# A planner that counts eight transfers in flight, with four of its durations changed, in a four-layer graph network

## The chip, the cores and the metric

The kernel runs on one core of one Trainium2 chip. The metric is the device time of one execution in microseconds (us); smaller is better. All data are 32-bit floats. In the profile PE is TensorE's matmuls, PEld its loads of weights, DVE VectorE, ACT ScalarE, POOL GpSimd, and SP SyncE, whose queue issues nearly all DMA transfers.

## The reference

128 graphs of 128 nodes with 512 features pass four layers. Each layer is `x = layernorm(x + f(x, adj))`, with another `f`; `adj` is a sparse 128 x 128 matrix for each graph. Cut to what matters:

```python
# layer 0: graph convolution over K = 3 hops, with attention weights
Xw = X @ Wv + bv
e = leaky_relu(sj[:, None, :] + si[:, :, None] + ab)         # sj, si: Xw @ aw
alpha = A * exp(e);  T = alpha / (alpha.sum(-1) + 1e-12)
for k in range(3):
    H = H + Xk @ Wk[k] + bk[k];  Xk = T @ Xk                 # f = relu(H)
# layer 1: two hypergraph convolutions, 512 -> 1024 -> 512
def conv(x, adj, W, b):                                      # H = adj != 0
    return Dn * (H @ (Be * (H.T @ (x @ W.T)))) + b           # Dn, Be: 1 / weighted degrees
h = layer_norm(relu(conv(x, adj, W1, b1))) * gamma + beta;  f = conv(h, adj, W2, b2) + x
# layer 2: tanh attention
s = (x @ w) @ a;  A = exp(leaky(8 * tanh((s_i + s_j) / 8))) * adj
A = A / A.sum(-1) * adj.sum(-1);  f = A @ x @ w
# layer 3: 8 heads of 64, scores times the mask 2 * adj, softmax
q, k, v = proj(x);  S = softmax(q @ k.T / 8 * (adj + adj));  f = (S @ v) @ Wo.T + bo
```

## The kernel before

**A program that is planned before it is issued.** The kernel's code does not issue instructions as it runs. Every call such as `ve.tensor_tensor(...)` goes to `Plan.add`, which notes the engine, an estimated duration (`estimate`), a key (`plan.key`, a due time in units of a pair of graphs), and on which earlier operations it depends. Some 90,000 instructions come out of it. At the end `Plan.emit` orders all of them, and each engine runs its own list strictly in that order. Since all instructions are issued from one line of `emit` (L375), the profile has one line for all; operations are told apart by the names of the buffers (`four`, `out`, `first`, `side`, `sq`, `bank`, `t`) that they write and read.

**How `Plan.order` works.** It is a list scheduler with a clock for each of the five engines. In each step it takes, for each engine, the operations whose inputs are ready; `look(e)` gives each the time `t` at which it could start, and among those that could start within `SLACK` = 60 ns of the earliest it takes the one of best rank. The rank is the key in the first pass; in two further passes it is a deadline worked back from the first pass's start times, for all engines but TensorE. Of the three orders the one with the shortest planned time is issued. An operation that takes a new buffer also needs a free slot in SBUF or PSUM, so the plan chooses the buffers too. An operation in a `plan.together()` block is planned as one piece: its durations are added, times a share given to `together`.

**Transfers in the plan.** A DMA keeps its queue for `ISSUE` = 450 ns an instruction; its data then go over one common pipe (`pipe`), 1000 ns (`BEGIN`) after the issue at the earliest, for a time worked out from the bytes and the runs (`o[7]`); operations that need the data become ready 2300 ns after the pipe's end (the last row of `LATENCY`). In the issued program, transfers use eight semaphores in turn, and each waits, in its issuing queue, until the transfer eight places ahead has landed. The plan before has no such limit.

**Ports in the plan.** An operation of POOL, or of DVE with two SBUF operands, shares a port (`shares_port`). When POOL ends, DVE's port is held `YIELD` = 20 ns longer.

**The stages.** Work goes in steps of two pairs of graphs (`both`), so 32 steps a layer. Large products are done by Strassen's method (`strassen`, and twice over in `twice`). In layer 0, the weighted `e` goes through DRAM to be turned (`through_dram`: writes in groups of four pieces of 16 KB, `e<-sq`, then one load, `sq<-e`), and the same is done in layer 1 with `h` and in layers 2 and 3 with `F`, `x` and `S`. Layer 1 loads `adj` in groups of four pieces (`sq<-in_adj_dram`) and counts nonzeros with `ve.tensor_scalar(..., accum_out=cnt)`. Layers 2 and 3 run in one function (`layer23`), which calls `attention`; it has 16 matmuls of scores in one `together` block (two of them on the upper and lower 64 rows of the array) and 16 matmuls with the values in another (two on halves of the columns). `dot` is a multiply-add on VectorE with `accum_out`, both operands in SBUF.

While layer 0 runs, the weights of later layers are combined and parked in DRAM (`park_49`, `park_7`: `w1s`, `w2s`, `qks` and others). Between the layers they are loaded into `first` (`take_49`, `take_w2`), a buffer that the weights of the layer before used, seven loads of 896 KB or 512 KB in a row.

Of the kernel before, what the change touches and what calls it, by code (L numbers as in the profile page):

```python
# [59 lines left out]
PE, DVE, ACT, POOL, SP = range(5)  # L60

LATENCY = ((0, 205, 215, 255, 300), (225, 120, 110, 200, 200), (160, 145, 140, 200, 200), (110, 140, 100, 105, 200),
           (2300, 2300, 2300, 2300, 2300))
ISSUE, BEGIN = 450, 1000
EARLY = -0.5
QW = 3 * P + 2
SLACK = 60
SPARE, AHEAD = 4, 6
YIELD = 20
SIZE = {"four": U * D, "sq": U * (P + 2), "bank": D, "col": 12, "row": D, "w28": 7168, "q7": 7 * 2 * P,  # L70
        "w7": 7 * QW, "out": U * 4 * QW, "t0": D, "t1": D, "row1": 4 * D, "k": U * (P + 2),
        "prep": U * D}
# [51 lines left out]
def estimate(engine, name, out, args, kw):  # L124

    n = out.idx.size if isinstance(out, View) else 0
    views = [a for a in args if isinstance(a, View)]
    psum = any(a.tile.kind in PSUM for a in views)
    scalars = sum(isinstance(a, View) and a.idx.size == 1 for k, a in [*enumerate(args), *kw.items()] if k != "accum_out")
    if engine == PE:  # L130
        return 107 if name == "transpose" else (1.74 if n <= P else 1.68) * n
    if name == "dma_start":
        return ISSUE
    if engine == DVE:
        if name == "bn_aggr":
            return 95
        if name == "reciprocal":
            return 67 + 6.5 * n
        if name in ("tensor_reduce", "bn_stats"):
            n = views[0].idx.size  # L140
        fast = name in ("tensor_scalar", "tensor_copy") and not psum and "accum_out" not in kw
        return 67 + n / (1.92 if fast else .96) + (61 * scalars if n > 8 else 0)
    if engine == ACT:
        return 50 + n / 1.2 + (0 if psum else 43) + 92 * scalars + 94 * ("accum_out" in kw)
    if name == "tensor_tensor":
        return 500 + 35 * n if OP.pow in args else 150 + 2.1 * n if n < 800 else 1.82 * n
    return 60 if name == "memset" else 180 + 3.2 * n if n > 8 else 215


def shares_port(engine, name, args, kw):  # L150
# [22 lines left out]
class Plan:  # L173
# [64 lines left out]
    def order(self, urgent=None):  # L238


        ops = self.ops
        n = len(ops)
        after = [[] for _ in range(n)]
        left = [len(o[4]) for o in ops]
        todo, first = {}, {}
        for k, o in enumerate(ops):
            for d in o[4]:
                after[d].append(k)
            for t in o[5]:
                todo[t] = todo.get(t, 0) + 1  # L250
                first[t] = min(first.get(t, o[3]), o[3])
        line = {kind: sorted((t for t in first if t.kind == kind), key=first.get, reverse=True) for kind in self.slots}
        slots = {kind: [(0, i) for i in range(m)] for kind, m in self.slots.items()}
        place = {}
        later = {new: (set(old), 0.0) for new, old in self.later.items()}

        def settle(kind):

            if line[kind] or kind not in {old[0] for olds in self.later.values() for old in olds}:
                return False  # L260
            found, slots[kind] = slots[kind], []
            for at, i in found:
                for new, (old, when) in list(later.items()):
                    if (kind, i) in old:
                        later[new] = rest, when = old - {(kind, i)}, max(when, at)
                        if not rest:
                            slots[new[0]].append((when, new[1]))
            return bool(found)

        rank = [o[3] if o[0] == PE or urgent is None else (urgent[k], k) for k, o in enumerate(ops)]  # L270
        ready = [{} for _ in range(5)]
        come, free, start = [0.0] * n, [0.0] * 5, [0.0] * n
        port = [0.0] * 5
        pipe, reached = 0.0, EARLY
        for k in range(n):
            if not left[k]:
                ready[ops[k][0]][k] = 0.0

        def look(e):

            can = []
            soonest = math.inf
            for k, t in ready[e].items():
                if e == SP and ops[k][8] > reached and not ops[k][4]:
                    continue
                t = max(t, free[e], port[e] if ops[k][6] else 0)
                new = {}
                for tile in ops[k][5]:
                    if tile not in place:
                        new.setdefault(tile.kind, []).append(tile)  # L290
                for kind, tiles in new.items():
                    s, m = slots[kind], len(tiles)
                    spare = 0
                    if not all(tile in line[kind][-m:] for tile in tiles):
                        spare = SPARE if all(tile in line[kind][-m - AHEAD:] for tile in tiles) else math.inf
                    if len(s) < m + (min(spare, 4) if kind == "bank" else spare):
                        break
                    t = max(t, sorted(s)[m - 1][0])
                else:
                    can.append((rank[k], t, k))  # L300
                    if t < soonest:
                        soonest = t
            if not can:
                return None
            r, t, k = min(c for c in can if c[1] <= soonest + SLACK)
            return t, k

        best = [look(e) for e in range(5)]
        count = 0
        while count < n:  # L310
            t, e = min((b[0], e) for e, b in enumerate(best) if b)
            k = best[e][1]
            o = ops[k]
            stale = {e}
            for tile in o[5]:
                if tile not in place:
                    s, l = slots[tile.kind], line[tile.kind]
                    at = min(s) if tile.place is None else next(x for x in s if x[1] == tile.place)
                    s.remove(at)
                    place[tile] = at[1]  # L320
                    l.remove(tile)
                    settle(tile.kind)
                    stale = set(range(5))
            del ready[e][k]
            start[k] = t
            free[e] = end = t + o[2]
            if o[7]:
                end = pipe = max(pipe, t + BEGIN) + o[7]
            if e == PE and o[8] > reached:
                reached = o[8]  # L330
                stale.add(SP)
            if o[6]:
                port[DVE + POOL - e] = end + (YIELD if e == POOL else 0)
                stale.add(DVE + POOL - e)
            count += 1
            for tile in o[5]:
                todo[tile] -= 1
                if not todo[tile]:
                    slots[tile.kind].append((end + max(LATENCY[SP if o[7] else e]), place[tile]))
                    settle(tile.kind)  # L340
                    stale = set(range(5))
            for j in after[k]:
                f = ops[j][0]
                come[j] = max(come[j], end + LATENCY[SP if o[7] else e][f])
                left[j] -= 1
                if not left[j]:
                    ready[f][j] = come[j]
                    stale.add(f)
            for f in stale:
                best[f] = look(f)  # L350
        return start, place, max(free)
# [32 lines left out]
def kernel(  # L384
# [14 lines left out]
    psum = ctx.enter_context(tc.tile_pool(name="psum", bufs=1, space=PS))  # L399
# [40 lines left out]
    plan = Plan(slots, later)  # L440
# [1015 lines left out]
    def attention(i0, A, qT, kT, v, x3d, base, r):  # L1456
# [4 lines left out]
        Ss = [four().rearrange("p u (j a) -> p (u j) a", a=Q).rearrange("p (k j) a -> p k j a", k=4)  # L1461
              for _ in range(U)]
        ps = [[bank(), bank()] for _ in range(U)]
        with plan.together(.65):
            for b in range(U):
                for i in range(C):
                    for r2 in range(2):
                        pe.matmul(ps[b][r2][:, i * P:(i + 1) * P],
                                  qT[r2 * HD:(r2 + 1) * HD, b, i],
                                  kT[r2 * HD:(r2 + 1) * HD, b, i], start=True, stop=True)  # L1470
# [33 lines left out]
            PTs.append(PT)  # L1504
        cT = four().rearrange("p u (i n) -> p u i n", n=P)
        ps = [bank() for _ in range(U)]
        with plan.together(.62):
            for b in range(U):
                for i in range(C):
                    for r2 in range(2):  # L1510
                        hh = (2 * i + r2) * HD
                        pe.matmul(ps[b][r2 * HD:(r2 + 1) * HD, i * P:(i + 1) * P], v[:, b, hh:hh + HD],
                                  PTs[b][:, r2, i * P:(i + 1) * P], start=True, stop=True)
        for b in range(U):
            ac.copy(cT[:, b].rearrange("p i (r m) -> p i r m", m=4), rows_in_order(ps[b]))
        ops = operands(*blocks(cT))
# [8 lines left out]
    n = B // U  # L1525
# [61 lines left out]
```

## Time and profile before

| what | value |
|---|---|
| runs | 5402.33, 5396.24, 5395.81 us; median 5396.24 |
| profiled execution | 5406.97 us, its span 5405.0 us |
| granted TensorE clock | 0.998 |
| busy PE / DVE / POOL / ACT | 5324.9 / 4410.1 / 3913.6 / 2387.5 us |
| DMA | 813.70 MB, mean 151 GB/s |
| instructions | 93,824 |

The page's "busy" time of an engine is the time in which at least one of its instructions runs; an instruction's record reaches somewhat into the next one's, since engines are pipelined. A 32-bit matmul has two records, one for each of its passes. In groups of instructions, the first numbers after the bar are total busy time and mean ns of one, then follow the idle time of the engine just before them and what ended it. A line of the waits gives total us, the number of waits and the longest. In the timeline the columns are start, length in us, engine, operation with buffers, and in brackets the engine's idle time before it with its releaser.

### The profile page before, as it was taken

The numbers are of one execution on the slowest core, as the hardware profiler recorded it, in microseconds if no ns is written. First come the engines' busy times: TensorE is split into PE (matmuls) and PEld (weight loads), VectorE is DVE, ScalarE is ACT, GpSimd is POOL, SyncE is SP. The second block draws the span as 40 slices with busy tenths as digits, with TensorE's granted clock in tenths as the row PEclk, the third lists the DMA queues.
The fourth block names the chain that finished last, engine by engine and source line by source line (L and its number), as shares of the span: only waits on it lengthen the run. The fifth ranks groups of instructions, "written<-read, shape, count | busy, mean of one in ns | idle before, by whom it ended". The sixth has DMA issues, their size and how long they took to land.

```text
span 5405.0 us, 93824 instructions
## 1 busy us (share of the span) xinstructions
PE 5324.9 (99%) x29039; PEld 4239.3 (78%) x29039; DVE 4410.1 (82%) x11721; ACT 2387.5 (44%) x6085; POOL 3913.6 (72%) x4937
## 2 busy tenths in 40 slices
PE   8999999999999999999999999999999999999998
PEld 4555555555788888888888889988988998998987
DVE  7788888887888888888888777878777878788886
ACT  3343333343444444444444444444444444444444
POOL 6777677676676767676767577777777777778776
PEclk9999999999999999999999999999999999999999
DMA  4444444435554545454554745555555555555543
GB/s 112 134 135 130 130 146 134 128 113 181 154 157 145 158 146 158 147 157 146 157 150 146 246 137 158 159 154 161 162 154 158 157 161 156 162 154 163 156 153 109
DMA packets 842412, 813.70 MB, mean 151 GB/s; under 512 B 269612, under 2 KB 642868, under 8 KB 841912
## 3 DMA queue, kind: packets, MB, share of 16 engines
q1 hardware_dynamic: 838914, 806.65, 49.2%
q8 instruction: 231, 3.78, 0.3%
q14 instruction: 269, 2.20, 0.1%
q10 hardware_dynamic: 2998, 1.06, 0.1%
HBM read 458.38 MB, written 349.04 MB: 149 GB/s over the span
## 4 chain that ended last, share of the span: by engine, by line
PE 87%; DVE 5%; DMA 3%; issue 1%; SPq 1%; ACT 1%; POOL 1%; ACTq 0%; DVEq 0%; POOLq 0%
PE bank L375 66%; PE t L375 21%; DVE out L375 1%; SPq L375 1%; DVE col L375 1%; DVE four L375 1%; DMA first<-x3d 1%; DMA four<-in_x_dram 1%; ACT out L375 0%; DMA out<-x3d 0%; DMA sq<-e 0%; POOL out L375 0%; DVE junk L375 0%; DVE first L375 0%; DMA sq<-in_adj_dram 0%
## 5 line engine op out<-in xcount | busy, mean ns | idle before, releaser
L375 PE MATMUL bank<-first,four 128*128 128x386 f32 (+2 forms) x6008 | 1735.6, 433 | 27.3 <-DVE out L375 11.4
L375 PEld LDWEIGHTS bank<-first,four 128*128 128x128 f32 (+1 forms) x6008 | 1073.0, 189 | 600.6 <-DVE out L375 119.2
L375 DVE TENSOR_TENSOR out<-bank,out 128x386 f32<-128x386 f32 (+1 forms) x2089 | 1011.2, 501 | 261.6 <-PE bank L375 197.3
L375 DVE TENSOR_TENSOR four<-bank,four 128x256 f32<-128x256 f32 x1285 | 529.5, 418 | 204.6 <-PE bank L375 176.6
L375 POOL TENSOR_TENSOR col<-col,neghalf 128x2 f32<-128x2 f32 x320 | 233.9, 731 | 374.6 <-DVE col L375 372.5
L375 POOL TENSOR_TENSOR out<-out 128x772 f32<-128x772 f32 (+3 forms) x233 | 328.0, 1416 | 219.4 <-DVE out L375 187.5
L375 POOL TENSOR_TENSOR four<-four 128x256 f32<-128x256 f32 (+2 forms) x448 | 362.5, 822 | 171.6 <-DVE four L375 110.4
L375 PE MATMUL bank<-first,out 128*128 128x256 f32 (+1 forms) x1912 | 458.6, 375 | 10.4 <-DVE four L375 6.2
L375 POOL TENSOR_TENSOR four<-four,four 128x256 f32<-128x256 f32 (+2 forms) x501 | 436.2, 876 | 11.7 <-DVE four L375 3.7
L375 ACT COPY out<-bank 128x258 f32<-128x258 f32 (+2 forms) x523 | 208.2, 403 | 481.6 <-PE bank L375 415.2
L375 PEld LDWEIGHTS bank<-first,out 128*128 128x128 f32 (+1 forms) x1912 | 340.6, 187 | 77.4 <-DVE four L375 13.1
L375 ACT ACTIVATE four<-four,col,col 128x512 f32<-128x512 f32 (+1 forms) x300 | 263.6, 905 | 153.8 <-POOL col L375 139.1
L375 PE MATMUL bank<-four,first 128*128 128x256 f32 (+3 forms) x1680 | 303.4, 324 | 6.9 <-DVE out L375 3.0
L375 PE MATMUL bank<-out,first 128*128 128x128 f32 (+2 forms) x1636 | 269.3, 300 | 2.5 <-DVE out L375 2.2
L375 PEld LDWEIGHTS bank<-four,first 128*128 128x128 f32 (+2 forms) x1680 | 237.8, 182 | 34.7 <-DVE out L375 5.4
L375 PE MATMUL t<-out,sq 128*128 128x512 f32 x512 | 258.0, 596 | 6.7 <-ACT t L375 4.8
L375 ACT ACTIVATE out<-out,col,col 128x512 f32<-128x512 f32 (+1 forms) x191 | 166.7, 901 | 193.6 <-POOL col L375 193.6
L375 ACT COPY t<-out 128x512 f32<-128x512 f32 x256 | 151.0, 591 | 225.5 <-DVE four L375 150.7
L375 DVE BATCH_NORM_STATS2 col<-four 128x6 f32<-128x512 f32 x368 | 244.7, 679 | 4.1 <-ACT four L375 1.7
L375 DVE TENSOR_TENSOR four<-t,four 128x256 f32<-128x256 f32 x435 | 181.4, 418 | 80.5 <-PE t L375 72.2
L375 PEld LDWEIGHTS bank<-out,first 128*128 128x128 f32 (+1 forms) x1636 | 224.9, 187 | 21.8 <-DVE out L375 2.6
L375 PE MATMUL t<-first,four 128*128 128x256 f32 (+1 forms) x902 | 232.5, 377 | 0.2 <-DVE four L375 0.2
(535 smaller groups left out, 13056.6 us busy)
## 6 DMA issues: line engine op xcount, KB each, us to landing
four<-h SPq DMA_DIRECT2D x72, 512.0 KB, 5.3
h<-four SPq DMA_DIRECT2D x272, 128.0 KB, 2.5
four<-in_x_dram SPq DMA_DIRECT2D x504, 64.0 KB, 2.1
four<-in_x_dram SPq DMA_DIRECT2D x61, 512.0 KB, 4.3
x1d<-four SPq DMA_DIRECT2D x61, 512.0 KB, 2.9
four<-x1d SPq DMA_DIRECT2D x61, 512.0 KB, 4.4
out<-x1d SPq DMA_DIRECT2D x54, 512.0 KB, 4.8
first<-S SPq DMA_DIRECT2D x54, 512.0 KB, 4.3
```

What stands on the lines that cost most here:

```text
L375: call(*map(real, args), **{n: real(a) for n, a in kw.items()})
```

## The change

Three things are altered in the planner, and nothing in what is computed.

First, `order` keeps the planned landing times of the last eight transfers (`landed`), of any queue: each transfer appends its pipe's end plus `LANDED` = 2050 ns. An operation of SP may start only when the places that it needs are free: its `j`-th instruction, which would be issued `450 * j` ns after its first, needs the landing of the transfer eight places ahead.

Second, `estimate` changes for two kinds of operation: a VectorE operation with `accum_out` and no PSUM operand gets 118 ns more, and a `tensor_scalar` of POOL with more than eight elements gets 740 ns less 160 for each scalar operand, in place of 180 + 3.2 ns an element.

Third, the shares of attention's two blocks of matmuls go from .65 to .558 and from .62 to .531, and `YIELD` from 20 to 0.

```diff
@@ -61,12 +61,12 @@
 
 LATENCY = ((0, 205, 215, 255, 300), (225, 120, 110, 200, 200), (160, 145, 140, 200, 200), (110, 140, 100, 105, 200),
            (2300, 2300, 2300, 2300, 2300))
-ISSUE, BEGIN = 450, 1000
+ISSUE, BEGIN, LANES, LANDED = 450, 1000, 8, 2050
 EARLY = -0.5
 QW = 3 * P + 2
 SLACK = 60
 SPARE, AHEAD = 4, 6
-YIELD = 20
+YIELD = 0
 SIZE = {"four": U * D, "sq": U * (P + 2), "bank": D, "col": 12, "row": D, "w28": 7168, "q7": 7 * 2 * P,
         "w7": 7 * QW, "out": U * 4 * QW, "t0": D, "t1": D, "row1": 4 * D, "k": U * (P + 2),
         "prep": U * D}
@@ -139,12 +139,13 @@
         if name in ("tensor_reduce", "bn_stats"):
             n = views[0].idx.size
         fast = name in ("tensor_scalar", "tensor_copy") and not psum and "accum_out" not in kw
-        return 67 + n / (1.92 if fast else .96) + (61 * scalars if n > 8 else 0)
+        slow = 118 if "accum_out" in kw and not psum else 0
+        return 67 + n / (1.92 if fast else .96) + (61 * scalars if n > 8 else 0) + slow
     if engine == ACT:
         return 50 + n / 1.2 + (0 if psum else 43) + 92 * scalars + 94 * ("accum_out" in kw)
     if name == "tensor_tensor":
         return 500 + 35 * n if OP.pow in args else 150 + 2.1 * n if n < 800 else 1.82 * n
-    return 60 if name == "memset" else 180 + 3.2 * n if n > 8 else 215
+    return 60 if name == "memset" else (740 - 160 * scalars if scalars else 180 + 3.2 * n) if n > 8 else 215
 
 
 def shares_port(engine, name, args, kw):
@@ -272,6 +273,7 @@
         come, free, start = [0.0] * n, [0.0] * 5, [0.0] * n
         port = [0.0] * 5
         pipe, reached = 0.0, EARLY
+        landed = [0.0] * LANES
         for k in range(n):
             if not left[k]:
                 ready[ops[k][0]][k] = 0.0
@@ -284,6 +286,8 @@
                 if e == SP and ops[k][8] > reached and not ops[k][4]:
                     continue
                 t = max(t, free[e], port[e] if ops[k][6] else 0)
+                if e == SP:
+                    t = max(t, *(landed[j - LANES] - ISSUE * j for j in range(len(ops[k][1]))))
                 new = {}
                 for tile in ops[k][5]:
                     if tile not in place:
@@ -326,6 +330,8 @@
             free[e] = end = t + o[2]
             if o[7]:
                 end = pipe = max(pipe, t + BEGIN) + o[7]
+                landed += [end + LANDED] * len(o[1])
+                landed = landed[-LANES:]
             if e == PE and o[8] > reached:
                 reached = o[8]
                 stale.add(SP)
@@ -1461,7 +1467,7 @@
         Ss = [four().rearrange("p u (j a) -> p (u j) a", a=Q).rearrange("p (k j) a -> p k j a", k=4)
               for _ in range(U)]
         ps = [[bank(), bank()] for _ in range(U)]
-        with plan.together(.65):
+        with plan.together(.558):
             for b in range(U):
                 for i in range(C):
                     for r2 in range(2):
@@ -1504,7 +1510,7 @@
             PTs.append(PT)
         cT = four().rearrange("p u (i n) -> p u i n", n=P)
         ps = [bank() for _ in range(U)]
-        with plan.together(.62):
+        with plan.together(.531):
             for b in range(U):
                 for i in range(C):
                     for r2 in range(2):
```

## Prediction

> **What bounds the kernel now.** I read the page first, for the engine that fills the span, then the same by stage, then the waits of that engine and of the DMA queue, then the timeline round the longest waits. From the page: busy time and the chain by engine.
>
> ```profile
> PE 5324.9 (99%) x29039; PEld 4239.3 (78%) x29039; DVE 4410.1 (82%) x11721; ACT 2387.5 (44%) x6085; POOL 3913.6 (72%) x4937
> ...
> PEclk9999999999999999999999999999999999999999
> ...
> PE 87%; DVE 5%; DMA 3%; issue 1%; SPq 1%; ACT 1%; POOL 1%; ACTq 0%; DVEq 0%; POOLq 0%
> ```
>
> TensorE is busy for 5324.9 of 5405.0 us at an undiminished clock, so a change of order alone, with the same instructions, can win back at most 80 us (1.5%). Where these 80 us lie is told by the busy time by stage (my cuts: start, layer 0, passage to layer 1, layer 1, passage to layers 2 and 3, these, end); the columns are length, then busy us and instructions of PE, PEld, DVE, ACT, POOL, then clock, DMA share and GB/s:
>
> ```profile
> 0.00:60.00 60.00, 42.36 (x88) 19.15 (x89) 37.12 (x86) 23.40 (x52) 29.25 (x40) 0.97 0.53 125
> 60.00:1300.00 1240.00, 1225.87 (x3664) 663.65 (x3663) 1013.60 (x2593) 481.64 (x1059) 915.71 (x1107) 1.00 0.44 128
> 1300.00:1420.00 120.00, 111.35 (x477) 80.83 (x476) 92.00 (x293) 55.53 (x102) 76.81 (x116) 0.96 0.66 209
> 1420.00:2960.00 1540.00, 1531.65 (x7374) 1302.34 (x7375) 1336.07 (x3696) 721.03 (x1202) 1053.85 (x1435) 1.00 0.50 153
> 2960.00:3180.00 220.00, 215.75 (x1211) 185.82 (x1210) 169.30 (x452) 88.70 (x193) 127.41 (x163) 1.00 0.58 189
> 3180.00:5260.00 2080.00, 2068.24 (x15228) 1873.39 (x15227) 1665.69 (x4369) 947.89 (x3243) 1615.34 (x1970) 1.00 0.52 158
> 5260.00:5405.00 145.00, 129.68 (x1006) 114.17 (x1004) 96.34 (x239) 69.27 (x236) 95.20 (x110) 0.98 0.35 111
> ```
>
> Length less PE's column gives PE's idle time: 17.6 us at the start, 14.1 in layer 0, 8.7 in the passage of 120 us, 8.4 in layer 1, 4.3 in the second passage, 11.8 in layers 2 and 3, 15.3 at the end. Start and end are filling and draining, so some 47 us are the planner's to win.
>
> Next, the DMA queue in the passage: what SyncE waited for there, and its timeline with the PE wait that followed.
>
> ```profile
> SPq L375 <- DMA first<-w1s: 9.2, 6, 2.1
> SPq L375 <- DMA first<-w2s: 5.3, 6, 1.1
> ```
>
> ```profile
> 1325.97 9.18 SPq L375 DMA_DIRECT2D sq<-in_adj_dram  x8
> ...
> 1341.85 0.37 SPq L375 DMA_DIRECT2D out<-x1d  x1
> 1343.09 9.81 SPq L375 DMA_DIRECT2D sq<-in_adj_dram  x8
> ```
>
> ```profile
> 1356.25 1.22 PE L375 MATMUL bank<-first,out 128*128 128x256 f32 x2 [3.08 <-DVE four L375]
> ```
>
> Eight small loads take 9.2 and 9.8 us to issue, where eight cost under 4 us elsewhere (e<-sq x8 at 586.90: 3.99 us): each waits for the landing of a transfer eight places ahead, here loads of 896 and 512 KB that don't concern it. TensorE then loses 3.08 us. A second place is 570 to 600 us, where parked weights are fetched: eight pieces of x take 6.99 us to issue, and the waits of PE in that window are 3.4 us for ACT t and 0.8 us for DVE out.
>
> **What the Trainium skill says.** "DMA: Bandwidth & Descriptors", section "Anatomy of one DMA", gives a fixed cost of some 2.0 us and says that a semaphore wait is taken by the issuing sequencer, not by the DMA engines. The trace agrees: 16 KB land 1.5 to 2.2 us after issue, and SyncE is what stands still. "TensorE: Matmul & The Clock Gate", part 3, "The mechanism", lets matmuls on different row groups run at once; the trace shows it below. "VectorE: DVE Perf Modes", section "Two Vector instructions with no wait between them", counts an operation with an accumulator output as two instructions; the trace has the second one, of 0.08 us.
>
> **The change, part by part.** No instruction is added or removed; the planner's clock changes, and with it the order and the buffers of everything. Each part is priced by how far the planner stood from the trace.
>
> *Attention's matmuls.* The planner takes 16 calls x 128 columns x 1.74 = 3564 ns, times the share. For the scores .65 gave 2316 ns and .558 gives 1988. The timeline:
>
> ```profile
> 3463.26 2.06 PE L375 MATMUL bank<-four,four 64*128 64x128 f32 x32
> 3465.25 0.94 PE L375 MATMUL t<-rows,first 128*128 128x128 f32 x6
> ```
>
> The next group begins 1.99 us on: .558 is right. For the values .62 gave 2209 and .531 gives 1892; 16 of its 32 records take 0.92 us (3424.36 to 3425.28), so it is right too. Each of 64 attentions was planned 0.33 + 0.32 = 0.65 us too long: 41 us in all, 2% of layers 2 and 3, in which TensorE ran ahead of its plan and met work not yet ready. TensorE itself gets no faster. Of that stage's 11.8 us idle I give 40% to this: **-4.7 us** (bounds: 0 and -11.8). What is late next is DVE's addition from a bank, which already ends most of PE's waits there.
>
> *GpSimd's tensor_scalar.* Planned 180 + 3.2 x 128 = 590 ns; now 580 with one scalar, 420 with two.
>
> ```profile
> L375 POOL TENSOR_SCALAR sq<-sq,col 128x128 f32<-128x128 f32 x256 | 155.3, 615 | 87.1 <-DVE col L375 86.4 <-DMA x1d<-four 0.6
> L375 POOL TENSOR_SCALAR sq<-sq,col,col 128x128 f32<-128x128 f32 x128 | 56.5, 452 | 79.7 <-DVE col L375 73.0 <-PE bank L375 4.4 <-DMA out<-x3d 2.3
> ```
>
> The recorded 615 and 452 overlap the next instruction a little, so both new values fit. 128 x 170 ns = 22 us of GpSimd's plan in a stage where it is busy 78%: hidden by that slack, so 0 (bound, were it all in front of PE: 22 us sooner in the plan, within the 11.8 us above on the chip).
>
> *118 ns more for VectorE with an accumulator and no PSUM operand.* It falls on the dot products (planned 600, now 718) and on layer 1's count of nonzeros (planned 200, now 318). In the timeline, dots begin at 585.54, 586.26 and the operation after them at 586.88: 720 and 620 ns. The counts:
>
> ```profile
> 1970.14 0.27 DVE L375 TENSOR_SCALAR_CACHE_REDUCE sq<-sq 128x128 f32<-128x128 f32 x1
> 1970.34 0.08 DVE L375 DVE_READ_ACCUMULATOR sq<-sq 128x1 f32 x1
> 1970.34 0.28 DVE L375 TENSOR_SCALAR_CACHE_REDUCE sq<-sq 128x128 f32<-128x128 f32 x1
> ```
>
> One follows the other after 200 ns: the old value was right there, and the new one is 118 too long, 128 times (15 us of 1540 in the plan). It is late on paper only; hidden by DVE's 13% of free time in layer 1: 0 (bounds +-4, half of that stage's idle time). YIELD at 0 takes 20 ns off some VectorE starts after GpSimd: no row shows it; less than any wait above, 0, with +-3 as bounds.
>
> *Eight in flight.* SyncE's next transfer now waits in the plan until the one eight earlier has landed: BEGIN 1000 + the time on the wire + LANDED 2050 ns. A 16 KB piece is 113 ns on the wire by the planner's formula, so 3.16 us; eight issues of 450 take 3.6, so small pieces never block each other. A 512 KB load is 1.51 us, an 896 KB one 2.54, and they queue behind each other: after them the plan blocks, as the chip does. So the plan learns of the two places above. Their idle time is 8.7 + 4.2 = 12.9 us; I expect 60% back, since the weights of layer 1 cannot be loaded before layer 0's buffer is free: **-7.7 us** (bounds: -12.9, and a loss as in the slower rival). Behind a blocked SyncE stand all later loads and stores, layer 0's e among them; TensorE waits for those through VectorE's transposes. ACT's transfers at the start fill places in the plan too but don't wait there, so the start may move: 0, bounds +-4.
>
> **Sum.** -4.7 - 7.7 = -12.4 us. The profiled execution took 5406.97 us (span 5405.0 and 2.0 around it): 5394.6. It stands 0.2% above the median of the three runs, 5396.24; scaled, the forecast is **5384 us**.
>
> **The rivals.** About 0.2% (10.8 us) is what a measurement of this kernel can tell from no change.
>
> *A new lottery, no change.* A list scheduler of this size reorders everything for a few ns, and a few waits of 1 us go away in one place and appear in another. For: layer 1 runs at 0.5% idle and its fault made worse. Against: two corrections meet waits that the trace shows. Time: 5396 +- 10.
>
> *Groups starve, slower.* A group of four small transfers needs four places, a single load one. In the plan, when the queue is full, a single's time is the first landing; a group's is the fourth less 1350 ns. With landings 1.51 us apart the group comes 3 x 1.51 - 1.35 = 3.2 us later, beyond the 60 ns in which urgency decides, so less urgent big singles pass it, and go on passing. The groups are layer 0's e and layer 1's adj and h, on which TensorE hangs. Place: the passage and the parked fetches. Price: one wait like those of 3.08 and 3.4 us, say 3.3, each time. For: SyncE waits there 12 times for w1s and w2s alone. Against: most of the time the places are not full. With eight such waits and the 7.7 us not won: 26.4 - 4.7 = +21.7, so 5418 us. From five on (5 x 3.3 - 4.7 = 11.8) it is slower by over 0.2%.
>
> *Better than forecast.* Three quarters of the 47 us go: -35, 5361 us. Against: most single waits of PE are under 1 us, spread over hundreds of microseconds.
>
> **How the numbers follow.** The forecast with its better neighbour 0.46, no change 0.30, starving groups or another bad order 0.24. These are the chances of faster, same and slower. The likeliest case alone runs from 5361 to 5390; to hold 8 in 10 the range reaches over no change into the slower case: 5360 to 5419.
>
> **What would show it.** Right: PE's busy time unchanged at 5325 +- 5 us; PE's idle time in the passage under 5 us of 120, and no 3.4 us wait near a parked fetch; idle time in layers 2 and 3 near 7 us; SyncE's waits for w1s and w2s no longer followed by a PE wait. Wrong: waits of PE over 2 us behind e, adj or h after large loads (starving), idle time in layer 1 above 12 us (the 118 ns), or a start that fills later than 60 us.

## The result, and the profile after

No change: 5397.68 us (median of 12 runs, 5393.1 to 5400.2) against 5396.45 us before (12 runs); ratio 1.000, 95% interval 0.9991 to 1.0009. The forecast was 5384 us, so 14 us too low; the time fell where the rival "a new lottery, no change" had put it. That is not how it came about: large effects of both signs cancel, as the experiments show.

One warning ahead. The profiled executions differ by more than the kernels do: before's took 5406.97 us, 10 above its median, after's 5396.67, 1 below. The two spans (5405.0 and 5394.1) look like a gain that the medians do not have. The stages are what to compare.

From the page of the changed kernel, busy times and the chain:

```profile
PE 5308.3 (98%) x29039; PEld 4233.2 (78%) x29039; DVE 4436.2 (82%) x11721; ACT 2403.0 (45%) x6085; POOL 3902.7 (72%) x4937
...
PE 88%; DVE 7%; issue 2%; DMA 1%; ACT 1%; POOL 1%; SPq 0%; ACTq 0%; DVEq 0%; POOLq 0%
```

DMA's share of the chain fell from 3% to 1% and VectorE's rose from 5% to 7%: waits for transfers were indeed traded for others. The same stages as before (length, busy time of PE, PEld, DVE, ACT, POOL with instructions, clock, DMA share, GB/s):

```profile
0.00:60.00 60.00, 36.40 (x74) 15.65 (x75) 34.78 (x79) 23.36 (x51) 29.77 (x46) 0.89 0.55 133
60.00:1300.00 1240.00, 1233.44 (x3702) 670.88 (x3701) 1027.36 (x2628) 479.83 (x1067) 916.23 (x1106) 1.00 0.44 129
1300.00:1420.00 120.00, 104.43 (x456) 76.76 (x454) 87.15 (x265) 51.77 (x95) 76.56 (x111) 0.93 0.61 194
1420.00:2960.00 1540.00, 1535.12 (x7410) 1308.38 (x7410) 1341.97 (x3704) 738.18 (x1211) 1053.34 (x1441) 1.00 0.51 153
2960.00:3180.00 220.00, 214.96 (x1229) 186.58 (x1228) 173.47 (x457) 91.32 (x215) 130.26 (x167) 1.00 0.60 194
3180.00:5260.00 2080.00, 2063.51 (x15280) 1867.70 (x15280) 1681.62 (x4369) 953.58 (x3227) 1607.56 (x1972) 1.00 0.51 158
```

PE's idle time (length less busy), before and after: start 17.6 and 23.6 us, layer 0 14.1 and 6.6, passage 8.7 and 15.6, layer 1 8.3 and 4.9, second passage 4.2 and 5.0, layers 2 and 3 11.8 and 16.5. Layers 0 and 1 gained 11 us; start, passage and the last stage lost 18.

The places that the forecast had named changed sides. Near 590 us, where parked weights are fetched, eight pieces of x now issue in 3.72 us (6.99 before), and TensorE's waits of 3.4 and 0.8 us between 570 and 600 us are gone. In the passage it is worse; the longest waits of PE there, then SyncE's timeline and PE's:

```profile
PE bank L381 <- POOL sq L381: 10.0, 1, 10.0
PE t L381 <- DVE sq L381: 2.5, 1, 2.5
```

```profile
1326.81 3.73 SPq L381 DMA_DIRECT2D first<-w2s  x5
...
1331.17 0.56 SPq L381 DMA_DIRECT2D four<-x1d  x1
1331.78 2.79 SPq L381 DMA_DIRECT2D sq<-in_adj_dram  x4
...
1339.22 4.70 SPq L381 DMA_DIRECT2D e<-sq  x8
1343.97 3.75 SPq L381 DMA_DIRECT2D sq<-in_adj_dram  x8
...
1348.24 5.77 SPq L381 DMA_DIRECT2D sq<-in_adj_dram  x12
```

```profile
1352.84 1.38 PE L381 MATMUL bank<-sq,sq 128*128 128x130 f32 x4 [10.05 <-POOL sq L381]
1354.01 3.43 PE L381 MATMUL t<-out,sq 128*128 128x512 f32 x4
```

The load of x1d behind the weights lands 9.45 us after its issue (in the chain of waits, 1331.17 to 1340.62), the pieces of adj behind it land with it, and the next small transfers wait for their places. Then SyncE issues some twenty small transfers one after another, to 1350.2, before the piece of adj that TensorE's chain waits for. The last line has a second price: four records of 512 columns take 3.43 us, where in the kernel before four take 1.98:

```profile
1334.87 1.98 PE L375 MATMUL t<-out,sq 128*128 128x512 f32 x4 [1.49 <-DVE col L375]
```

After the long wait TensorE runs at half its rate for a while; its granted clock is 0.50 from 1352 to 1356 us and 0.93 over the stage.

At the start, TensorE's first real work comes at 22.44 us, not 15.99 (the kernel before, then the changed one):

```profile
15.99 2.91 PE L375 MATMUL bank<-first,four 128*128 128x386 f32 x4 [6.19 <-DVE four L375]
22.44 8.26 PE L381 MATMUL bank<-first,four 128*128 128x386 f32 x18 [12.66 <-DVE four L381]
```

### The profile page after: what moved, and what is told of

Its sections match the earlier page's. It is cut to its first block, busy times and chain, and to the rows that moved or that the text cites. A ratio compares the mean times of both kernels' runs of the same rounds, so it can differ in the third digit from the quotient of the medians.

```text
span 5394.1 us, 93993 instructions
## 1 busy us (share of the span) xinstructions
PE 5308.3 (98%) x29039; PEld 4233.2 (78%) x29039; DVE 4436.2 (82%) x11721; ACT 2403.0 (45%) x6085; POOL 3902.7 (72%) x4937
## 4 chain that ended last, share of the span: by engine, by line
PE 88%; DVE 7%; issue 2%; DMA 1%; ACT 1%; POOL 1%; SPq 0%; ACTq 0%; DVEq 0%; POOLq 0%
PE bank L381 69%; PE t L381 20%; DVE out L381 1%; DVE four L381 1%; DVE first L381 1%; DVE col L381 1%; DVE junk L381 1%; SPq L381 0%; DVE side L381 0%; ACT out L381 0%; POOL four L381 0%; DMA four<-x1d 0%; POOL first L381 0%; ACT four L381 0%; DVE rows L381 0%
## 5 line engine op out<-in xcount | busy, mean ns | idle before, releaser
L381 DVE TENSOR_TENSOR out<-bank,out 128x386 f32<-128x386 f32 (+1 forms) x1999 | 969.9, 504 | 245.3 <-PE bank L381 178.9
L381 POOL TENSOR_TENSOR out<-out 128x772 f32<-128x772 f32 (+2 forms) x262 | 359.1, 1380 | 265.9 <-DVE out L381 188.6
L381 DVE TENSOR_TENSOR four<-bank,four 128x256 f32<-128x256 f32 x1025 | 421.6, 418 | 131.8 <-PE bank L381 122.6
L381 PE MATMUL bank<-first,out 128*128 128x256 f32 x1850 | 458.6, 380 | 1.2 <-DVE four L381 0.6
L381 PEld LDWEIGHTS bank<-first,out 128*128 128x128 f32 x1850 | 345.2, 190 | 62.3 <-issue 10.5
L381 DVE TENSOR_TENSOR first<-bank,first 128x256 f32<-128x256 f32 (+1 forms) x601 | 242.7, 416 | 104.4 <-PE bank L381 90.3
L381 PE MATMUL bank<-four,first 128*128 128x128 f32 (+3 forms) x1848 | 292.6, 302 | 1.7 <-DVE out L381 0.9
L381 PE MATMUL bank<-first 128*128 128x128 f32 (+1 forms) x1972 | 256.0, 277 | 1.5 <-DVE out L381 1.1
L381 PEld LDWEIGHTS bank<-first 128*128 128x128 f32 (+1 forms) x1972 | 231.6, 182 | 15.8 <-issue 5.8
L381 PE MATMUL t<-first,four 128*128 128x256 f32 (+2 forms) x1052 | 237.9, 356 | 2.5 <-DVE four L381 1.2
```

Of the source, the lines that this page charges most:

```text
L381: call(*map(real, args), **{n: real(a) for n, a in kw.items()})
```

## The experiments

**Theory A:** the edits act on separate stages, each with a sign of its own, and the sum is near zero; a stage's steady pattern follows from the settings that hold in that stage. **Theory B:** every edit deals a new order, and nothing carries over from one kernel to another. All kernels keep the computation whole. The table collects them; times on different chips compare by the ratio to the kernel before, measured beside each. Idle is PE's, in us, by the windows above, from one profiled execution each. The kernel before took 5396.05 to 5401.59 us (medians) on the chips used; whether a time lies in an expected range is told by the time as measured. Where expectations give 7.7 and 9.3 us for passage and layer 1 of the kernel before, the table has 8.7 and 8.3: the same sum.

| kernel | median us | ratio (95% interval) | start | layer 0 | passage | layer 1 | layers 2, 3 |
|---|---|---|---|---|---|---|---|
| before | 5396.45 | 1 | 17.6 | 14.1 | 8.7 | 8.3 | 11.8 |
| after | 5397.68 | 1.000 (0.9991-1.0009) | 23.6 | 6.6 | 15.6 | 4.9 | 16.5 |
| lanes_only | 5392.89 | 0.9988 (0.9981-0.9995) | 23.5 | 9.0 | 12.2 | 4.4 | 9.3 |
| durations_only | 5376.76 | 0.9961 (0.9946-0.9976) | 16.6 | 10.2 | 7.9 | 10.4 | 3.9 |
| shares_only | 5418.47 | 1.0038 (1.0023-1.0053) | 16.4 | 12.2 | 13.7 | 6.3 | 23.7 |
| yield_only | 5423.20 | 1.0048 (1.0033-1.0063) | 16.8 | 13.1 | 9.9 | 6.1 | 31.6 |
| places_past_start | 5386.40 | 0.9973 (0.9962-0.9984) | 16.9 | 7.3 | 11.9 | 4.5 | 15.6 |
| places_l0_l1 | 5369.83 | 0.9939 (0.9924-0.9954) | 16.7 | 7.6 | 13.1 | 4.7 | 3.8 |
| durations_no_118 | 5382.87 | 0.9962 (0.9949-0.9975) | 16.9 | 13.0 | 8.7 | 5.5 | 10.1 |
| durations_yield20 | 5410.11 | 1.0015 (1.0009-1.0022) | 17.1 | 12.3 | 10.9 | 6.5 | 21.4 |
| passage_rate | 5374.71 | 0.9959 (0.9944-0.9973) | 17.0 | 7.0 | 15.9 | 4.2 | 4.1 |
| places_l23 | 5391.28 | 0.9991 (0.9983-1.0000) | 17.0 | 10.0 | 9.5 | 7.7 | 14.5 |
| places_l0_l1_old | 5389.08 | 0.9986 (0.9979-0.9993) | 17.0 | 6.5 | 16.0 | 7.0 | 11.3 |
| yield_10 | 5373.44 | 0.9957 (0.9941-0.9974) | 16.9 | 7.6 | 7.0 | 5.4 | 12.2 |

### The count alone

The diff of the change without its lines on `estimate`, the shares and `YIELD`.

> The kernel before with the eight places alone; durations, shares and YIELD as before. Theory A (two real effects that cancel): the count of places takes the long waits out of layer 0 and worsens the start and the passage. Then PE's idle time is near the changed kernel's in these three stages: 60 to 1300 us 6 to 9 us (before 14.1), start 22 to 25 (before 17.6), passage 12 to 17 (before 7.7), while layers 1 and 2 and 3 stay within 3 us of before (9.3 and 11.8); time 5394 to 5402. Theory B (a new lottery): the stage figures agree with neither kernel, and layers 1 to 3 move as much as layer 0.

Measured 5392.89 us. Start 23.5, layer 0 9.0 and passage 12.2 came as A said. Layer 1 fell to 4.4, more than the 3 us that A allowed, and the time lies 1 us under A's range. For figures near the changed kernel's in these stages the count alone suffices. Layers 2 and 3 have the count here too, and stand at 9.3, below before's 11.8.

### The durations alone

```diff
-                if e == SP:
+                if False:
                     t = max(t, *(landed[j - LANES] - ISSUE * j ...))
```

> The changed kernel without its count of places, durations, shares and YIELD as changed. Theory A: start, layer 0 and passage as before (17.6, 14.1, 7.7 us of PE idle time, each within 3), layers 2 and 3 as in the changed kernel: regular waits of 0.35 to 0.4 us, two in each 71.7 us, in sum 15 to 18, and 55 pairs of graphs in 1973 us (before 1979); time 5384 to 5393, since the losses of the count are absent. Theory B: no stage like either kernel, time 5388 to 5406.

Measured 5376.76 us, 0.39% under before, and layers 2 and 3 with 3.9 us of idle time, not the changed kernel's 16.5. A was right on start and passage, missed layer 0 by 1 us (10.2, where 14.1 less 3 was its limit) and was wrong on this stage and on the time. The regular waits there in the changed kernel, two in each 71.5 us and of 0.2 to 0.3 us (not 0.35 to 0.4, as expected above), are not the durations' doing alone. They are not the count's alone either: lanes_only has the count in this stage and not these waits. The changed kernel, then lanes_only, from 3180 to 5260 us:

```profile
PE bank L381 <- DVE col L381: 3.4, 17, 0.2
PE bank L381 <- DVE col L381: 1.2, 1, 1.2
```

They come with the count and the new durations together.

### The two shares alone

```diff
-        with plan.together(.65):
+        with plan.together(.558):
-        with plan.together(.62):
+        with plan.together(.531):
```

> The kernel before with the two shares of attention's matmuls alone changed (.558, .531). My prediction's step: 4.7 us less idle time in layers 2 and 3 (11.8 before), so about 7, and a time near 5391. Theory A by the changed kernel's trace: idle time there isn't lower (12 to 17 us), but the waits are short and regular and 55 pairs take 1972 to 1976 us, 3 to 6 us less than before. Theory B: waits irregular as before, 1976 to 1984 us.

Measured 5418.47 us: slower by 0.38%, against my forecast of a gain and against both theories' figures. VectorE's, GpSimd's and PE's timelines show one of the waits, which come back eleven times, 144 to 147 us apart:

```profile
4173.07 1.76 DVE L375 SCALAR_TENSOR_TENSOR junk<-ks,row 128x512 f32<-128x512 f32 x1
4174.77 0.08 DVE L375 DVE_READ_ACCUMULATOR junk<-ks,row 128x1 f32 x1
4174.88 1.63 DVE L375 SCALAR_TENSOR_TENSOR junk<-ks,row 128x512 f32<-128x512 f32 x1
```

```profile
4173.01 1.28 POOL L375 TENSOR_TENSOR first<-four,first 128x512 f32<-128x512 f32 x1
4174.24 1.71 POOL L375 TENSOR_TENSOR first<-four,out 128x512 f32<-128x512 f32 x1
4176.03 1.74 POOL L375 TENSOR_TENSOR first<-first 128x256 f32<-128x256 f32 x2
```

```profile
4177.33 1.37 PE L375 MATMUL bank<-out,first 128*128 128x256 f32 x4 [2.04 <-DVE out L375]
4178.49 1.91 PE L375 MATMUL bank<-four,four 128*128 128x256 f32 x4
4180.20 1.64 PE L375 MATMUL bank<-out,four 128*128 128x256 f32 x4
4181.68 1.03 PE L375 MATMUL bank<-four,four 128*128 128x256 f32 x4
```

Two dot products planned at 600 ns take 1.76 and 1.63 us, each until shortly after an operation of GpSimd ends; the addition that TensorE needs stands behind them. The page "SBUF — State Buffer" of the Trainium skill, section "SBUF: two separate sides", calls the port pair that GpSimd shares with VectorE's operations on two SBUF inputs an exclusive lock, for which the loser waits; these lines agree. And again the wait costs more than its 2.04 us: the next groups of four records take 1.91 and 1.64 us, then 1.03 as usual. TensorE's plan was made right here, and the time rose: in the new order these dots meet GpSimd's operations just ahead of an addition that TensorE needs.

### YIELD alone

```diff
-YIELD = 20
+YIELD = 0
```

> The kernel before with YIELD at 0 in place of 20 ns, nothing else: the smallest of the edits, to learn how far the time moves when the order is merely dealt anew. Theory A: stages move by up to 3 us each and the time stays within 6 us of before. Theory B (the lottery is what decides): at least one stage moves by 5 us or more, and the time by up to 10 us either way.

Measured 5423.20 us: 0.48% slower by 20 ns. Start, layers 0 and 1 and the passages moved by less than 3 us each, as A had it; layers 2 and 3 went from 11.8 to 31.6 us, as B had it; the time moved by more than twice what either theory allowed. The waits there, some 0.2 to 1.8 us each, are spread over VectorE's operations, the most costly being:

```profile
PE bank L375 <- DVE first L375: 8.4, 12, 1.8
PE bank L375 <- DVE four L375: 6.7, 9, 1.2
PE bank L375 <- DVE out L375: 5.3, 10, 0.8
```

### The count past the start, and in two halves

```diff
-                if e == SP:
+                if e == SP and ops[k][8] > 0:            # places_past_start
+                if e == SP and 0 < ops[k][8] < 129:      # places_l0_l1
+                if e == SP and ops[k][8] >= 129:         # places_l23
```

> The changed kernel, its count of places applied to operations with a key over 0 alone, so not to the loads of the first microseconds. Theory A (the count has two faults, at the start and in the passage, and two gains, in layers 0 and 1): PE's idle time at the start 16 to 18 us as with no count (16.6; changed kernel 23.6), layers 0 and 1 as in the changed kernel (6.6 and 4.9, within 3 each), passage still 12 to 17; time 5386 to 5393. Theory B (each edit deals a new order and nothing carries over): a stage far from the start moves by 8 us or more, layers 2 and 3 above all, time 5375 to 5420.

Measured 5386.40 us, inside A's range, every stage as A said but for a passage of 11.9, just under its 12 to 17. Taking the count from the start is worth 0.27% of the time (1.0000 less 0.9973): 15 us. The profiles show where: idle time at the start is 6.7 us less, its clock is 1.00 and not 0.89, which over 60 us is worth up to 6.6 us (an estimate from these clocks), and the passage, though it kept the count, has 3.7 us less.

> The changed kernel with the count applied to layers 0 and 1 alone (keys between 0 and 129): start and layers 2 and 3 are planned as without it. Theory A: start 17, layer 0 about 7 to 9, layer 1 about 5, layers 2 and 3 about 4 (as with the durations alone, 3.9), passage 8 to 16; time 5366 to 5376, better than the durations alone (5376.8). Theory B: layers 2 and 3 fall into some other pattern, idle 4 to 32 us as in the six kernels so far, time 5370 to 5410.

Measured 5369.83 us, inside A's range and 0.61% under before: this version beats both kernels. Layers 2 and 3, with the count gone from them:

```profile
3180.00:5260.00 2080.00, 2076.18 (x15385) 1896.07 (x15384) 1675.44 (x4404) 964.99 (x3256) 1624.60 (x1985) 1.00 0.52 159
```

3.8 us of 2080 are idle, and TensorE does 105 records more in the same window than in the changed kernel.

> The changed kernel with the count for keys from 129 on alone, so in layers 2 and 3 only. Theory A (the gain of the shares and durations there is eaten by the count): idle in layers 2 and 3 13 to 18 us with two waits of some 0.38 us in 71.7 us, start 16.6, layer 0 about 10, passage about 8, layer 1 about 10, all as with the durations alone; time 5384 to 5392. Theory B (chance): layers 2 and 3 in yet another pattern.

Measured 5391.28 us; 14.5 us of idle time in layers 2 and 3, with small regular waits as A had it (24 for DVE col, 13 for DVE first), though of 0.2 us and not 0.38. Three kernels with new durations have the count there: 16.5, 15.6, 14.5. Three have none: 3.9, 3.8, 4.1. So with the new durations the count costs some 11 us of idle time in that stage; with the old ones it cost none (9.3 in lanes_only, 11.8 before). Passage and layer 1 stand at 9.5 and 7.7, 1.5 over and 2.3 under A's figures.

### Old durations with the count in layers 0 and 1

The edit of places_l0_l1 with every duration, share and YIELD as before.

> The kernel before with the count in layers 0 and 1 alone, all durations and YIELD old. Theory A (stages are planned apart and add up): layer 0 7 to 9.5 us idle, layer 1 about 4.5, start 17.6, layers 2 and 3 about 12 as before; time 5380 to 5388, that is 7 to 12 us less than before by the count. Theory B (how layers 2 and 3 are entered deals their pattern anew): idle there 4 to 32 us, time 5372 to 5410.

Measured 5389.08 us, 1 us over A's range; ratio 0.9986. Layer 0 fell to 6.5, but layer 1 only to 7.0, and the passage, of which A had said nothing, rose to 16.0. Layers 2 and 3 nearly keep before's 11.8 (11.3), though layers 0 and 1 ahead of them were ordered anew: here, how the stage was entered did not deal its pattern.

### Which duration matters

```diff
-        return 67 + n / (...) + (61 * scalars if n > 8 else 0) + slow
+        return 67 + n / (...) + (61 * scalars if n > 8 else 0)         # durations_no_118
-YIELD = 0
+YIELD = 20                                                             # durations_yield20
```

> The kernel with the durations alone, less the 118 ns of VectorE's accumulating operations (shares, GpSimd's tensor_scalar and YIELD as changed). With the shares alone, TensorE waited 2.0 to 2.2 us in each 144 us for two dot products of 1.6 us each, planned at 0.6. Theory A (the longer dots in the plan are what takes this wait away): the wait of some 2 us comes back, idle in layers 2 and 3 18 to 28 us, time 5390 to 5415. Theory B (any new order may or may not have it): no such wait, time anywhere from 5370 to 5420. Theory C, that GpSimd's or YIELD's value did it: idle stays 3 to 7 us, time 5372 to 5380.

Measured 5382.87 us; the ratio, 0.9962, equals that with the 118 ns (0.9961). Idle time in layers 2 and 3 is 10.1, between A's figure and C's, with three waits of 1.6 to 1.7 us; layer 1's is 5.5 instead of 10.4. Neither A nor C fits, and B allowed almost any time. With the 118 ns one stage has less idle time and the other more. So the gain of the durations does not rest on the 118 ns.

> The kernel with the durations alone, but YIELD back at 20 ns. In the kernel before, YIELD alone cost 24 us (5423.2), nearly all in layers 2 and 3. Theory A (durations that are right make the plan sturdy): idle time in layers 2 and 3 stays 3 to 8 us, time 5373 to 5383. Theory B (the steady pattern of layers 2 and 3 is drawn anew by 20 ns): idle there moves by 8 us or more, time 5385 to 5420.

Measured 5410.11 us. B was right: with YIELD at 20 the gain of the durations is gone, 21.4 us idle in layers 2 and 3, though every duration is the new one.

> The kernel with the count in layers 0 and 1 alone (5369.8 us), YIELD at 10 in place of 0. Layers 0 and 1, start and passage within 3 us each by either theory. Theory A (layers 2 and 3 are sturdy with right durations): 3 to 8 us idle there, 5367 to 5376. Theory B (they are dealt anew by 10 ns, as YIELD at 20 did): 10 us or more, 5378 to 5405.

Measured 5373.44 us, in A's range, but by accident: layers 2 and 3 rose to 12.2 us (B), and the passage fell to 7.0 from 13.1, which neither theory allowed. A planner setting of 10 ns moves single stages by 6 to 8 us.

### The passage with slower transfers in the plan

```diff
+            moved *= 1.5 if 61 < self.key < 69 else 1
```

> The kernel with the count in layers 0 and 1 alone (5369.8 us), and in it the planned time on the wire times 1.5 for operations with keys between 61 and 69, which are the loads of layer 1's weights and their neighbours. The plan takes 1.44 us for a 512 KB load of w2s; in the changed kernel seven of them took 15 us, 2.1 each. Theory A (the remaining wait of 5 to 10 us in the passage comes from transfers that are slower there than planned): PE's idle time in the passage falls from 13.1 to 4 to 8 us, the rest stays within 3 us a stage, time 5361 to 5367. Theory C (the passage must wait for the weights whatever the order): passage stays 10 to 15 us, time 5366 to 5374.

Measured 5374.71 us, passage 15.9 us: A fell, and C's figures, 5374 us and 15 us at most, were both missed by 1 us. The seven loads of w2s went out in one row (1308.03, 6.96 us), the groups of e behind them took 8.85 us to issue, and TensorE waited 6.4 and 4.1 us, both times for VectorE's `sq`; in the chain the first comes by way of e, the second by way of adj. What order would shorten the passage stays open.

## Why the prediction came out as it did

**Right, with luck in the size.** That the count would take idle time out of layer 0: it is 10.0 to 14.1 us in the seven kernels without the count there and 6.5 to 9.0 in the seven with it. Near 590 us the mechanism is as forecast: the group that stood in the queue goes out in half the time, and the wait of 3.4 us is gone. TensorE has a wait of over 2 us there, from 593 to 598 us, in five of the seven kernels without the count and in none with it. For the layer as a whole the mechanism is not shown. By the semaphores in the traces (instructions of SyncE for which the landing eight places ahead came last), SyncE stood before a full queue in layer 0 for 5.8 to 10.8 us in the kernels without the count, and for 11.5 to 16.7 us in those with it. TensorE lost less, though SyncE stood longer. The size agrees by luck: of the 7.7 us forecast two thirds were to come from the passage, which gave nothing, and the 7.5 us with old durations (places_l0_l1_old, 0.14%) come from elsewhere. With new durations it is 7 us by the times and 12 by the ratios (0.9961 to 0.9939, whose intervals overlap). That layer 1's 118 ns would bring no net gain by themselves came true as well (0.9961 with them, 0.9962 without); GpSimd's figure was never tried by itself.

**Wrong, where the gain would lie.** 8.7 of the 12.9 us at stake were placed in the passage. It did not shrink: 7.9 to 13.7 us without the count, 7.0 to 16.0 with it. The step that failed is the one from SyncE's waits to TensorE's. The count did shorten SyncE's waits for w1s and w2s between 1300 and 1420 us, from 14.0 to 16.6 us in the kernels without it to 6.3 to 12.0 in six of the seven with it. In durations_only and in places_l0_l1, which differ by the count alone:

```profile
SPq L381 <- DMA first<-w1s: 8.7, 6, 2.0
SPq L381 <- DMA first<-w2s: 5.5, 6, 1.2
...
SPq L381 <- DMA first<-w1s: 6.8, 4, 2.0
SPq L381 <- DMA first<-w2s: 2.4, 4, 1.1
```

Yet PE's idle time in the passage rose from 7.9 to 13.1 us. Small loads that are issued earlier get stuck behind the weights all the same: in the changed kernel the pieces of adj landed with x1d, 9 us after their issue, where the median for such a piece is 2.4. In the kernel before, x1d behind the weights took 10.73 us. The gain came in layer 0, and in layer 1, for which the forecast had no term of the count: 5.5 to 10.4 us idle without it and 4.2 to 7.0 with it.

**Mis-sized, the start.** "0, bounds +-4" is 15 us by places_past_start. The two kernels with the count at the start have 23.5 and 23.6 us of idle time there, the twelve others 16.4 to 17.6. The plan lets SyncE wait for places that ACT's transfers take, but not ACT; SyncE's order changes, and the first work of TensorE comes 6.45 us later, at a clock of 0.89 instead of 0.97. That ACT's exemption causes it was argued from the code, not tried.

**Mis-sized, the durations.** 4.7 us, with 11.8 as the outer bound, are 21 us (0.39%) for shares, durations and YIELD together. The 4.7 us were the shares' own, and the shares by themselves lost 20 us: a plan that is right for TensorE alone did not bring back idle time. The bound was wrong too, since it took PE's idle time for all that could be won. PE's busy time is not fixed by the work. It is 5324.9 us before and 5308.3 after, with the same matmuls; part of this may be the slow profiled execution of the kernel before, but yield_only with 5321.5 and places_l0_l1 with 5303.4 were both profiled within 2 us of their medians. Matmuls at half rate count as busy, and so must waits shorter than the overlap of two records; how much is due to each was not separated. "PE's busy time unchanged at 5325 +- 5" failed for the same reason.

**Missed, the count in layers 2 and 3.** It had no term. With the new durations it takes back 0.34% (places_l0_l1 to places_past_start), 18 us. SyncE stands before a full queue there for 1.6 us in the whole stage of the kernel before, by the same count from the semaphores, so there was little to win; why the count does harm with new durations and none with old ones is open. The planned 3.16 us for a small piece that lands in 1.5 to 2.4 (medians of e and adj) may be why, but this was not tried.

**Mis-sized, YIELD.** "0, with +-3" is +26 us alone (ratio 1.0048) and -29 us in company (1.0015 to 0.9961). It is no matter of 20 ns. In the plan an operation of GpSimd that is ready starts when the one before it ends, 20 ns ahead of a waiting VectorE, and takes the port again; at 0 a tie goes to VectorE. The dots above show VectorE getting its turn between two of GpSimd's operations. This reading of the code is argued; what is measured is the size, and that its sign turns with the durations.

The sum, from ratios, in one order of steps: durations with YIELD -0.39%, count in layers 0 and 1 -0.22%, count in layers 2 and 3 +0.34%, count at the start +0.27%: 0.00%. Each step is measured on top of the one before it, so they must add up to the whole; the sizes hold in this order only. On the old durations the whole count gains 0.12% (lanes_only), and the durations on top of it lose 0.12%. Adding the count at the start and in layers 2 and 3 to that in layers 0 and 1 changes the ratio by 0.02% with old durations (0.9986 to 0.9988) and by 0.61% with new ones (0.9939 to 1.0000). A prediction that adds up parts, as this one did, cannot give that.

**The rivals.** "A new lottery" gave the number. Against it stands that start, layer 0 and the last stage repeat from kernel to kernel where the settings are the same; for it, that settings of 10 or 20 ns move the last stage by 8 to 20 us, in either direction, and that the parts do not add. One cause of such jumps was not looked at: which of the planner's three orders each kernel issued is not on record, and a switch between them could deal every stage anew. "Groups starve" has a likeness in the passage, a 10 us wait behind large loads, but its mechanism, singles passing groups in the plan, was not tested. Its price of 3.3 us a wait left out the half rate that often follows.

## What to carry to other kernels

When a planner's order is issued as it stands, try its settings together as well as one by one: the shares alone made this kernel 20 us slower, YIELD alone 26, and both with GpSimd's figure made it some 21 us faster, with the 118 ns or without. Which pair does it is open, since the shares with YIELD were not run without GpSimd's figure. Put a resource limit into a plan stage by stage, and judge it by the time: here it gained in layers 0 and 1 and lost at the start and, with new durations, in layers 2 and 3, while the passage, where the trace showed most waits at the limit, gained nothing. Whether it should hold for every queue that uses the places was not tried. A net of zero is no proof that nothing happened: switch the change on by stage before it is dropped.

## What the runs showed of the hardware

A wait of TensorE of about 2 us can cost nearly twice its length. Between 60 and 5260 us of the fourteen profiles, after waits of 1.8 to 2.5 us matmuls ran at half rate (start to start 1.7 to 2.15 times the usual, four or more of them in the next 6 us) in 11 of 20 cases, after longer ones in 19 of 23, with some 1.6 us lost each time; after the 76 waits of 1 to 1.8 us, in none. It is the granted clock that falls. In shares_only, after the wait that ended at 4177.33 us and after the like one that ended at 4323.3 us:

```profile
4178.00:4182.00 4.00, 4.00 (x12) 3.21 (x12) 2.86 (x6) 0.00 (x0) 1.19 (x2) 0.57 0.00 0
4324.00:4328.00 4.00, 4.00 (x23) 3.53 (x21) 4.00 (x10) 0.00 (x0) 1.21 (x2) 1.00 0.01 2
```

The mean clock of these 4 us is 0.57 after a wait of 2.04 us and 1.00 after one of 1.97 us. Of the eleven waits of this pattern, 1.89 to 2.06 us long, seven were followed by the half rate and four were not, so length alone does not decide it; these seven are most of the 11 cases above. "TensorE: Matmul & The Clock Gate", part 1, gives some 3.4 us of idling before the clock halves; here 2 us sufficed about half the time.

The second surprise is how exactly a pattern repeats in layers 2 and 3. In shares_only a wait of 1.9 to 2.1 us returns eleven times, 144 to 147 us apart, and in the changed kernel two waits of 0.2 to 0.3 us return every 71.5 us, some 25 times each, so that one misplaced operation is paid for many times over.
